# Two scatters of half rows, attention inside 64 tiles, a PSUM tile per chunk, and a residual on another engine in a two-layer float32 kernel

## The chip, the cores and the metric

The kernel runs on one core of one Trainium2 chip. The metric is the device time of one execution in microseconds (us), and of several executions the median. The engines are named as the profile names them: PE is TensorE (PEld its loading of weights), DVE is VectorE, ACT is ScalarE, POOL is GpSimd, SP is SyncE, which here issues most of the transfers. A Q behind a name (SPq, POOLq) is the engine's queue of instructions.

## What is computed

Two layers over 2048 tokens of 512 channels, all in float32. Each layer normalises x, computes a branch s and a branch g from it, and adds s * silu(g). In layer 0, s is a gated recurrence over the tokens and g an expert layer in which every token takes one of two experts. In layer 1, s is an attention whose keys are pooled over blocks of 64 tokens except for the last 256, and g is an expert layer with two shared experts and four of sixteen routed ones for each token. Cut to what matters here:

```python
x = L0_attn_x                                  # (1, 2048, 512)
xn = _layernorm(x)
s = _L0_attn_ref(xn, ...)                      # recurrence, projections Wk, Wv, Wr, then Wo
g = _silu(_L0_ffn_ref(xn, ...))                # the better of E = 2 experts, FF = 2048
x = x + s * g
xn = _layernorm(x)
s = _L1_attn_ref(xn, ...)                      # 16 heads, 28 pooled keys + the last 256
g = _silu(_L1_ffn_ref(xn, ...))                # below
x = x + s * g

def _moe_forward(u, shared_w1, ..., centroids, bias):
    flat = u.reshape(-1, d)
    h = relu(einsum('td,ndf->ntf', flat, shared_w1) + shared_b1[:, None, :])
    out = flat + einsum('ntf,nfd->td', h, shared_w2) + shared_b2.sum(0)
    scores = sigmoid(flat @ centroids.T) + bias
    vals, idx = top_k(scores, 4)               # 4 of 16 experts
    gating = vals at idx, divided by their sum
    for each expert: rout += (relu(flat @ w1 + b1) @ w2 + b2) * gating   # D_FF = 352
    return out + rout
```

## The kernel before the change

Tokens stand in 16 tiles of 128 (P = 128, NT = 16, D = 512, NC = 4 chunks of channels). A scheduler in the build orders the instructions of each engine by what depends on what and by the order in which the program emits them, so the order of emission is a wish, except where `tc.keep_in_program_order` fixes an instruction. Each engine then works through its own list in order: an instruction that waits holds up all behind it on that engine. A named tile in a pool has `bufs` buffers; a writer of a buffer waits for the readers of what stood in it. Transfers from SP go out in SP's order. The stages, in order of time:

**Start (0 to about 73 us).** The 16 tiles of x are loaded, and `norm_stats` (L121) gives mean and 1/deviation of each on VectorE with a square root on ScalarE. The loop at L222 copies both into `facts` (L229, L230), normalises in place, transposes and stores the rows. From them follow the tables that say which token goes to which of layer 0's experts; `tok` and `row_mr` (L357, L358) come last.

**Layer 0 (to about 943 us).** Two pieces of work are interleaved by hand. `pieces0` (L583) runs the expert layer on gathered rows: `rows0` (L538) gathers by an indirect transfer from GpSimd, normalises on VectorE, transposes on TensorE (L558); `up0` (L562) makes the up-projection (L567) and its activation, `down0` the down-projection (L589). `recurrence(b)` (L384) is a generator over eight blocks of 256 tokens in 22 pieces each: differences and mixes, the projections of `wk`, `wv`, `wr` (L414), scans, the normalisation. The loop at L688 takes a piece of the recurrence whenever its share of the work lags behind `pieces0`.

**Between the layers (to about 1062 us).** `carried` (L698) multiplies by Wo (L705). VectorE multiplies by the gate (L832, L838), which ScalarE makes from rows `yg` that GpSimd gathers (L825). Then, for each pair of tiles, GpSimd adds x (L847), the sum is stored to `xr1`, and VectorE normalises it (L126, L854). TensorE transposes it into `xT` (L137) and multiplies by the centroids (L863).

**Routing, shared experts, keys (to about 1350 us).** Tables place each of the 8192 answers (2048 tokens x 4) in tiles of 128 rows, each tile of one expert: 64 full ones and up to 16 more, NRT = 80; how many there are is known only while the kernel runs (`tiles_n`, 73 in this input). 64 scatters from GpSimd (L1036), two streams of them under way at a time, put the rows into `xs` in DRAM. `down_shared` (L1092) stores the shared experts' sums, with the normalised x added, into `comb` in DRAM (L1105).

**Routed tiles (1350 to about 1908 us).** The loop at L1722 runs j from 0 to 80. `hidden_rows(j)` (L1648) loads the tile's rows x and its expert's weights (704 + 512 + 192 + 2 KB), transposes (L1669), copies (L1671) and multiplies in three chunks of 128, 128 and 96 hidden channels into one PSUM tile `ph` (L1672, L1676), each followed by a ReLU on ScalarE (L935, through `relu`); VectorE makes the weight of each row and the row `to` to which its answer goes (L1694; six buffers). `down_rows` (L1697) of the tile before multiplies down into `py` (L1700); VectorE scales it into `y` (L1705; four buffers), and GpSimd scatters it with addition into `comb` (L1706). All those scatters write one tensor, so each waits until the one before has landed. From j = 65 on a step runs only if the tile exists (L1726).

**Attention** over the first 14 tiles of tokens is a generator of 42 pieces (L1589): queries (L1342), scores (L1550, L1556) with a softmax on VectorE and ScalarE (L1312), and values (L1575, L1583) that overwrite `xT`. 34 pieces are spread over the first 72 steps; the rest run behind the loop, where `close(i)` closes a tile of tokens between them: silu of its sum on ScalarE (L1757), times `xT` and plus `xo` on VectorE (L1759, L1762), store (L1763). The loads of the sums from `comb` (L1752) wait for every scatter.

The lines that the scatter rests on:

```python
        nc.vector.tensor_scalar(out=y, in0=py, scalar1=g, scalar2=None, op0=ALU.mult)      # L1705
        nc.gpsimd.indirect_dma_start(                                                     # L1706
            out=comb, out_offset=bass.IndirectOffsetOnAxis(ap=to, axis=0),
            in_=y, in_offset=None, compute_op=ALU.add,
        )
...
            if j <= FULL_TILES and min(j + 1, SPREAD) * AHEAD // SPREAD > taken:          # L1728
                next(att)
                taken += 1
```

## Time and profile before

| what | us |
|---|---|
| median of 3 runs | 1981.36 (1971.8 to 1984.02) |
| the profiled execution | 1987.46 |
| its span in the profile | 1985.8 |
| TensorE busy in the span | 1869.7 (94%) |
| VectorE, ScalarE, GpSimd busy | 779.6, 531.4, 371.4 |

The page gives, for each engine, busy time and a strip of 40 slices of 49.6 us each, a digit being the busy share in tenths; a strip of the clock granted to TensorE and one of the DMA engines' mean busy share stand beside them:

```profile
PE   5899999999999999999889999999999999999857
...
POOL 1211121120302120200621560001111121221120
PEclk9799999999999999999899999999999999999989
DMA  7647786536562535346532551028999999998944
```

Lines of instruction groups name the line, the engine, the operation, what it writes and reads, and the count; behind the bar stand the busy time in us, the mean of one in ns, and the idle time of the engine just before them with what ended it. Lines of waits name who waited for whom, the sum in us, the times and the longest. Timeline lines give the start, the duration, engine and line, and in brackets the idle time before with its releaser. A matmul in float32 appears as two records; the ends of matmuls are modelled.

### The profile page before, as it was taken

What the parts mean: (1) busy time and instruction counts of PE and PEld (TensorE: products, weight loads), DVE (VectorE), ACT (ScalarE), POOL (GpSimd) and SP (SyncE); (2) the same over time, 40 slices, a digit from 0 to 9 for tenths busy, and PEclk for the clock granted to TensorE, in tenths of its full rate; (3) what the DMA queues carried; (4) which work ended last, traced back from release to release, by engine and by line L of the source; (5) the groups of instructions that cost most, each with busy time, mean ns of one, the idle gap of its engine ahead of it and who ended that gap; (6) DMA issues with size and microseconds to landing.
All of it is one profiled execution on the core that took longest, in us unless ns stands there. A gap on an engine that the chain in (4) does not pass through costs nothing.

```text
span 1985.8 us, 23193 instructions
## 1 busy us (share of the span) xinstructions
PE 1869.7 (94%) x8107; PEld 1294.9 (65%) x8107; DVE 779.6 (39%) x1580; ACT 531.4 (27%) x1001; POOL 371.4 (19%) x293
## 2 busy tenths in 40 slices
PE   5899999999999999999889999999999999999857
PEld 4677777777877787777334644446776666676634
DVE  8444545362627263440256444502322222222117
ACT  5113132322324232321423122221222222222214
POOL 1211121120302120200621560001111121221120
PEclk9799999999999999999899999999999999999989
DMA  7647786536562535346532551028999999998944
GB/s 249 230 148 243 240 268 219 190 106 191 168 214 89 167 95 163 113 138 228 191 111 89 213 187 58 32 75 269 278 306 273 292 286 264 259 276 234 278 90 160
DMA packets 199488, 381.35 MB, mean 192 GB/s; under 512 B 15804, under 2 KB 106428, under 8 KB 198472
## 3 DMA queue, kind: packets, MB, share of 16 engines
q1 hardware_dynamic: 179800, 332.78, 50.8%
q0 software_dynamic: 18272, 45.62, 9.9%
q10 hardware_dynamic: 1296, 1.41, 0.2%
q8 instruction: 67, 1.10, 0.2%
q14 instruction: 53, 0.43, 0.1%
HBM read 294.04 MB, written 85.72 MB: 191 GB/s over the span
## 4 chain that ended last, share of the span: by engine, by line
PE 66%; DMA 21%; DVE 5%; issue 4%; POOL 2%; ACT 2%; SPq 0%; POOLq 0%; DVEq 0%; ACTq 0%
PE pg L567 23%; DMA comb<-y,to 17%; PE py L589 11%; PE proj L414 7%; PE py L1098 4%; PE ph L1676 4%; PE ph L949 3%; PE py L1700 3%; PE pw L1583 1%; PE pl L863 1%; PE pq L1342 1%; PE pw L1467 1%; PE pq L1398 1%; POOL xr L847 1%; PE po L1458 1%
## 5 line engine op out<-in xcount | busy, mean ns | idle before, releaser
L567 PE MATMUL pg<-xg,w 128*128 128x256 f32 (+1 forms) x2304 | 494.9, 367 | 0.0
L567 PEld LDWEIGHTS pg<-xg,w 128*128 128x128 f32 x2304 | 419.0, 190 | 90.1 <-issue 41.6
L1676 PEld LDWEIGHTS ph<-xg,w 128*128 128x128 f32 (+1 forms) x1776 | 224.3, 185 | 128.6 <-ACT ht L935 64.2
L1676 PE MATMUL ph<-xg,w 128*128 128x128 f32 (+1 forms) x1776 | 245.5, 282 | 29.3 <-ACT xg L1671 14.4
L589 PE MATMUL py<-wd,hT 128*128 128x512 f32 x544 | 256.9, 593 | 3.0 <-DVE hT L574 3.0
L1700 PE MATMUL py<-w,ht 128*128 128x512 f32 (+1 forms) x438 | 219.7, 602 | 0.0
L1706 POOL DMA_INDIRECT comb<-y,to x73 | 113.8, 1559 | 459.9 <-DVE to L1694 279.9
L574 DVE TENSOR_TENSOR hT<-sg,pg 128x256 f32<-128x256 f32 (+1 forms) x144 | 57.0, 401 | 329.9 <-ACT sg L572 329.8
L572 ACT ACTIVATE sg<-pg 128x256 f32<-128x256 f32 (+1 forms) x144 | 53.4, 371 | 412.2 <-PE pg L567 411.9
L935 ACT ACTIVATE ht<-ph,b1t 128x128 f32<-128x128 f32 (+1 forms) x222 | 81.1, 365 | 296.0 <-PE ph L1676 286.7
L589 PEld LDWEIGHTS py<-wd,hT 128*128 128x128 f32 x544 | 102.1, 190 | 72.2 <-issue 61.9
L1705 DVE TENSOR_SCALAR y<-py,g 128x512 f32<-128x512 f32 x73 | 54.5, 747 | 157.2 <-PE py L1700 104.6
L1694 DVE TENSOR_TENSOR to<-junk,away 128x1 int32<-128x1 f32 x74 | 11.8, 159 | 221.7 <-DMA comb<-y,to 220.9
L1098 PE MATMUL py<-w,hT 128*128 128x512 f32 (+1 forms) x192 | 89.3, 596 | 0.0
L1700 PEld LDWEIGHTS py<-w,ht 128*128 128x128 f32 (+1 forms) x438 | 72.2, 194 | 25.8 <-issue 24.4
L949 PE MATMUL ph<-xT,w 128*128 128x512 f32 (+1 forms) x192 | 88.0, 597 | 0.1
L1036 POOL DMA_INDIRECT xs<-acc,slot x64 | 63.4, 991 | 69.2 <-DMA xs<-acc,slot 45.5
L1671 ACT COPY xg<-tp 128x512 f32<-128x512 f32 x74 | 43.2, 584 | 101.6 <-PE tp L1669 99.2
L705 PE MATMUL po<-wo,yb 128*128 128x512 f32 x128 | 61.6, 637 | 8.4 <-DVE acc L838 4.4
L414 PE MATMUL proj<-xm,wk 128*128 128x256 f32 x256 | 59.4, 386 | 3.6 <-DVE xm L404 3.6
L1342 PE MATMUL pq<-xT,wqg 128*128 128x256 f32 x224 | 56.9, 390 | 5.5 <-PEq L1724 5.5
L414 PE MATMUL proj<-xm,wv 128*128 128x256 f32 x256 | 61.5, 394 | 0.0
(416 smaller groups left out, 2180.7 us busy)
## 6 DMA issues: line engine op xcount, KB each, us to landing
w<-in_w_dram SPq DMA_DIRECT2D x76, 704.0 KB
w<-in_w_dram SPq DMA_DIRECT2D x76, 512.0 KB
w<-in_w_gate_dram SPq DMA_DIRECT2D x72, 512.0 KB
w<-in_w_up_dram SPq DMA_DIRECT2D x72, 512.0 KB
wd<-in_w_down_dram SPq DMA_DIRECT2D x72, 512.0 KB
xs<-zero SPq DMA_DIRECT2D x16, 1360.0 KB
x<-xs SPq DMA_DIRECT2D x74, 272.0 KB
w<-in_w_dram SPq DMA_DIRECT2D x76, 192.0 KB
```

The lines of the kernel that those rows point to most:

```text
L414: nc.tensor.matmul(out=ps[:, j, :], lhsT=w_[:, c, (o0 + j) * P : (o0 + j + 1) * P], rhs=xm[:, c, :], start=(c == 0), stop=(c == NC - 1),)
L567: nc.tensor.matmul(out=pg[:, i, 0:n], lhsT=w[:, c, i * FH + f * P : i * FH + (f + 1) * P], rhs=xg[:, c, 0:n], start=(c == 0), stop=(c == N ...
L589: nc.tensor.matmul(out=p, lhsT=hT[:, u * P : (u + 1) * P], rhs=wd[:, f, :], start=first_, stop=last_,)
L705: nc.tensor.matmul(out=po, lhsT=yb[:, c, s * P : (s + 1) * P], rhs=wo[:, c, :], start=(c == 0), stop=(c == NC - 1),)
L935: nc.scalar.activation(dst, src, AF.Relu, bias=b)
L949: nc.tensor.matmul(out=ph[0:n, :], lhsT=up(w, f, n, c), rhs=xT[:, c, cols], start=(c == 0), stop=(c == NC - 1),)
L1036: ins = nc.gpsimd.indirect_dma_start(out=xs, out_offset=bass.IndirectOffsetOnAxis(ap=slot[:, i, k : k + 1], axis=0), in_=acc[:, i, :], in_ ...
L1098: nc.tensor.matmul(out=py, lhsT=hT[0:n, e, f, s * P : (s + 1) * P], rhs=down(w, f, n), start=(e == 0 and f == 0), stop=(e == NS - 1 and f ...
L1342: nc.tensor.matmul(out=pq[:, j, :], lhsT=w[:, c, w0 : w0 + P], rhs=xT[:, c, tc0], start=(c == 0), stop=(c == NC - 1),)
L1676: nc.tensor.matmul(out=ph[0:n, f, :], lhsT=up(w, f, n, c), rhs=xg[:, c, :], start=(c == 0), stop=(c == NC - 1),)
L1700: nc.tensor.matmul(out=py, lhsT=hT[0:n, f, :], rhs=down(w, f, n), start=(f == 0), stop=(f == NF1 - 1),)
L1706: nc.gpsimd.indirect_dma_start(out=comb, out_offset=bass.IndirectOffsetOnAxis(ap=to, axis=0), in_=y, in_offset=None, compute_op=ALU.add,)
```

## The change

The parts of it:

- `comb` becomes two tensors of 256 channels each. `down_shared` stores each tile in two transfers, `down_rows` scatters each answer by two indirect transfers from GpSimd, one into each, and the closing loads each tile in two.
- All 42 pieces of attention run in the first 64 steps, spread evenly. The loads of `xo` move to steps 48 to 63. The closing of the 16 tiles stands in one loop behind all tiles, in the order of the tokens.
- `ph` is a PSUM tile of its own for each of the three chunks, from the same pool of two buffers.
- The residual add between the layers (L847) goes from GpSimd to VectorE.
- At the start, 1/deviation is written into `facts` at once and the means are copied once for all tiles (15 small copies fewer). Seven pieces of the recurrence are emitted ahead of `pieces0`, and the first transpose of gathered rows (L558) is kept in program order.

```diff
@@ -107,7 +107,8 @@
     dram = ctx.enter_context(tc.tile_pool(name="rows", bufs=1, space=bass.MemoryType.DRAM))
     xs = dram.tile([NRT * P, DX], F32, name="xs")
 
-    comb = dram.tile([T + P, D], F32, name="comb")
+
+    comb = [dram.tile([T + P, D // 2], F32, name=f"comb{h}") for h in range(2)]
     xnt0 = dram.tile([P, NC, T], F32, name="xnt0")
     ys0 = dram.tile([NST * P, D], F32, name="ys0")
     yr0 = dram.tile([NRB, P, NC * RB], F32, name="yr0")
@@ -118,14 +119,15 @@
         i = VEC.index(name)
         return vecs[:, i, c : c + 1]
 
-    def norm_stats(src, n):
-
-        mv = small.tile([P, n, 2], F32, tag=f"mv{n}", name="mv")
+    def norm_stats(src, n, mv=None, rstd=None):
+
+        if mv is None:
+            mv = small.tile([P, n, 2], F32, tag=f"mv{n}", name="mv")
+            rstd = small.tile([P, n], F32, tag=f"rstd{n}", name="rstd")
         for i in range(n):
             st = small.tile([P, 6], F32, tag="bnst", name="st")
             nc.vector.bn_stats(out=st, in_=src[:, i, :])
             nc.vector.bn_aggr(out=mv[:, i, :], in_=st)
-        rstd = small.tile([P, n], F32, tag=f"rstd{n}", name="rstd")
         nc.scalar.activation(rstd, mv[:, :, 1], AF.Sqrt, bias=eps)
         nc.vector.reciprocal(out=rstd, in_=rstd)
         return mv, rstd
@@ -218,16 +220,15 @@
         out=eno, in0=col[:, 0:NST], scalar1=float(P), scalar2=None, op0=ALU.mult
     )
 
+    all_mv = n0.tile([P, NT, 2], F32, bufs=1, name="all_mv")
     dl = n0.tile([P, NT], F32, bufs=1, name="dl")
     for i in range(0, NT, 2):
         xin = xins[i // 2]
-        mv, rstd = norm_stats(xin, 2)
+        mv, rstd = norm_stats(xin, 2, all_mv[:, i : i + 2, :], facts[:, 2, i : i + 2])
         shift = small.tile([P, 2], F32, tag="shift", name="shift")
         nc.vector.scalar_tensor_tensor(
             out=shift, in0=mv[:, :, 0], scalar=-1.0, in1=rstd, op0=ALU.mult, op1=ALU.mult
         )
-        nc.vector.tensor_copy(facts[:, 1, i : i + 2], mv[:, :, 0])
-        nc.vector.tensor_copy(facts[:, 2, i : i + 2], rstd)
         for j in range(2):
             xn = xin[:, j, :]
             nc.scalar.activation(
@@ -246,6 +247,7 @@
     wr = rc.tile([P, NC, D], F32, name="wr")
     tc.keep_in_program_order(nc.sync.dma_start(out=wv, in_=a["Wv"]))
     tc.keep_in_program_order(nc.sync.dma_start(out=wr, in_=a["Wr"]))
+    nc.vector.tensor_copy(facts[:, 1, :], all_mv[:, :, 0])
 
     sel = n0.tile([P, NT, E0], F32, bufs=1, name="sel")
     nc.vector.tensor_scalar(
@@ -555,7 +557,9 @@
         for u, xr in enumerate(xrs):
             tp = f0t.tile([P, NC, P], F32, tag="tp", name="tp")
             for c in range(NC):
-                nc.tensor.transpose(tp[:, c, :], xr[:, c * P : (c + 1) * P], ident)
+                ins = nc.tensor.transpose(tp[:, c, :], xr[:, c * P : (c + 1) * P], ident)
+                if u == c == 0 and js[0] == 0:
+                    tc.keep_in_program_order(ins)
             nc.scalar.copy(xg[:, :, u * P : (u + 1) * P], tp)
             yield
 
@@ -685,6 +689,9 @@
     WORK = NST * NPART * NFH - SLACK
     sh = ExitStack()
     after, spent = None, 0
+    for _ in range(7):
+        next(blocks)
+        done += 1
     for amount in pieces0():
         spent += amount
         while after is None and done * WORK < spent * PIECES * NRB:
@@ -844,7 +851,7 @@
         nc.sync.dma_start(out=xr, in_=a["x"][rows2, :].rearrange("(n p) d -> p n d", p=P))
         i0 = b * n
         for s in range(n):
-            nc.gpsimd.tensor_tensor(
+            nc.vector.tensor_tensor(
                 out=xr[:, s, :], in0=xr[:, s, :], in1=acc[:, i0 + s, 0:D], op=ALU.add
             )
         nc.sync.dma_start(out=xr1[rows2, :].rearrange("(n p) d -> p n d", p=P), in_=xr)
@@ -1102,7 +1109,10 @@
                     )
             y = m1s.tile([P, D], F32, tag="y", bufs=3, name="y")
             nc.vector.tensor_tensor(out=y, in0=py, in1=acc[:, t, 0:D], op=ALU.add)
-            nc.sync.dma_start(out=comb[t * P : (t + 1) * P, :], in_=y)
+            for h, c_ in enumerate(comb):
+                nc.sync.dma_start(
+                    out=c_[t * P : (t + 1) * P, :], in_=y[:, h * D // 2 : (h + 1) * D // 2]
+                )
 
     next(block)
 
@@ -1603,7 +1613,6 @@
 
         def value(i):
             values(i, got.pop(i))
-            finished.append(i)
 
         for b in range(nb - 1):
             q = start(b)
@@ -1669,15 +1678,15 @@
             nc.tensor.transpose(tp[:, c, :], x[:, c * P : (c + 1) * P], ident)
         xg = m1x.tile([P, NC, P], F32, tag="xg", name="xg")
         nc.scalar.copy(xg, tp)
-        ph = m1ps.tile([P, NF1, P], F32, tag="ph", name="ph")
         hT = hts[j % len(hts)]
         for f, n in enumerate(FCH):
+            ph = m1ps.tile([P, P], F32, tag="ph", name="ph")
             for c in range(NC):
                 nc.tensor.matmul(
-                    out=ph[0:n, f, :], lhsT=up(w, f, n, c), rhs=xg[:, c, :],
+                    out=ph[0:n, :], lhsT=up(w, f, n, c), rhs=xg[:, c, :],
                     start=(c == 0), stop=(c == NC - 1),
                 )
-            relu(hT[0:n, f, :], ph[0:n, f, :], b1t[0:n, j, f : f + 1])
+            relu(hT[0:n, f, :], ph[0:n, :], b1t[0:n, j, f : f + 1])
 
         junk = m1x.tile([P, NR], F32, tag="junk", name="junk")
         g = m1x.tile([P, 1], F32, tag="g", name="g")
@@ -1703,16 +1712,16 @@
             )
         y = m1x.tile([P, D], F32, tag="y", bufs=4, name="y")
         nc.vector.tensor_scalar(out=y, in0=py, scalar1=g, scalar2=None, op0=ALU.mult)
-        nc.gpsimd.indirect_dma_start(
-            out=comb, out_offset=bass.IndirectOffsetOnAxis(ap=to, axis=0),
-            in_=y, in_offset=None, compute_op=ALU.add,
-        )
+
+        for h, c_ in enumerate(comb):
+            nc.gpsimd.indirect_dma_start(
+                out=c_, out_offset=bass.IndirectOffsetOnAxis(ap=to, axis=0),
+                in_=y[:, h * D // 2 : (h + 1) * D // 2], in_offset=None, compute_op=ALU.add,
+            )
 
     FULL_TILES = T * KR // P
-    AHEAD = 34
-    SPREAD = FULL_TILES + NR // 2
-    finished = []
-    att = attention()
+    att = list(range(6 * (FULL[0] * P // QB)))
+    attend = attention()
     rest_of = {}
     held = nc.values_load(
         tiles_n[0:1, 0:1], min_val=FULL_TILES, max_val=NRT,
@@ -1721,39 +1730,36 @@
     pending, taken = None, 0
     for j in range(NRT + 1):
 
-        with contextlib.ExitStack() as step:
+        with contextlib.ExitStack() as more:
             if j > FULL_TILES:
-                step.enter_context(tc.If(held > j - 1))
+                more.enter_context(tc.If(held > j - 1))
             made = hidden_rows(j) if j < NRT else None
-            if j <= FULL_TILES and min(j + 1, SPREAD) * AHEAD // SPREAD > taken:
-                next(att)
+            if taken < len(att) and (j + 1) * len(att) // FULL_TILES > taken:
+                next(attend)
                 taken += 1
             if pending is not None:
                 down_rows(*pending)
             pending = (j, *made) if made is not None else None
-        if j > FULL_TILES and min(j + 1, SPREAD) * AHEAD // SPREAD > taken:
-            next(att)
-            taken += 1
-        i = j - (NRT - NT)
-        if 0 <= i < NT:
-            xo = fin.tile([P, D], F32, tag="xo", name="xo")
-            nc.sync.dma_start(out=xo, in_=xr1[i * P : (i + 1) * P, :])
-            rest_of[i] = xo
+            i = j - (FULL_TILES - NT)
+            if 0 <= i < NT:
+                xo = fin.tile([P, D], F32, tag="xo", name="xo")
+                nc.sync.dma_start(out=xo, in_=xr1[i * P : (i + 1) * P, :])
+                rest_of[i] = xo
+    assert next(attend, None) is None
 
     tiles.close()
     fin2 = ctx.enter_context(tc.tile_pool(name="fin2", bufs=NT))
 
 
     sums_of = {}
-    early = list(FULL) + list(finished)
-    todo = early + [i for i in range(NT) if i not in early]
-    for i in todo:
+    for i in range(NT):
         y = fin2.tile([P, D], F32, tag="y", name="y")
-        nc.sync.dma_start(out=y, in_=comb[i * P : (i + 1) * P, :])
+        for h, c_ in enumerate(comb):
+            nc.sync.dma_start(
+                out=y[:, h * D // 2 : (h + 1) * D // 2], in_=c_[i * P : (i + 1) * P, :]
+            )
         sums_of[i] = y
-
-    def close(i):
-        y = sums_of[i]
+    for i, y in sums_of.items():
         nc.scalar.activation(y, y, AF.Silu)
         y4 = y.rearrange("p (c t) -> p c t", t=P)
         nc.vector.tensor_tensor(
@@ -1761,15 +1767,6 @@
         )
         nc.vector.tensor_tensor(out=y, in0=y, in1=rest_of[i], op=ALU.add)
         nc.sync.dma_start(out=a["out"][i * P : (i + 1) * P, :], in_=y)
-
-    closed = 0
-    for u, _ in enumerate(att):
-        if u >= 2:
-            for i in early[closed : closed + 2]:
-                close(i)
-                closed += 1
-    for i in todo[closed:]:
-        close(i)
 
 
 # ---- launch: one core; the host lays the inputs out, and adds what the shapes alone decide ----
```

## The prediction

> **What bounds the kernel now.** I read the page's slices first, then the waits of the stretch in which the routed tiles run, then stretches, then the timeline where a stall stood out. TensorE is busy 94% of the span, so a change counts only where it takes work or a stall off TensorE, or shortens the end, where TensorE waits. The routed tiles run from 1350 to 1908 us, the end from there to 1985.8. In the slices the DMA is nearly full there too, but two other lines tell more:
>
> ```profile
> L1706 POOL DMA_INDIRECT comb<-y,to x73 | 113.8, 1559 | 459.9 <-DVE to L1694 279.9 <-DMA comb<-y,to 95.9 <-DMA w<-in_w_dram 15.6
> ...
> L1036 POOL DMA_INDIRECT xs<-acc,slot x64 | 63.4, 991 | 69.2 <-DMA xs<-acc,slot 45.5 <-DVE acc L1027 19.6 <-issue 4.1
> ```
>
> The 73 scatters of answers (L1706) occupy GpSimd for 114 us and idle it for 460: each waits until the one before has landed, since all add into one tensor. Issues run from 1368.1 to 1924.6, 7.7 us apart on the mean. Who waits behind it, between 1355 and 1846:
>
> ```profile
> POOL comb L1706 <- DVE to L1694: 265.7, 43, 8.0
> ...
> DVE to L1694 <- DMA comb<-y,to: 212.8, 45, 8.3
> ...
> PE ph L1676 <- ACT xg L1671: 14.4, 4, 6.4
> ```
>
> `to` has six buffers; when the scatters fall behind, VectorE stands at L1694 until an old one lands. How that reaches TensorE, once per softmax that is caught behind it:
>
> ```profile
> 1493.73 0.16 DVE L1694 TENSOR_TENSOR to<-junk,away 128x1 int32<-128x1 f32 x1 [7.35 <-DMA comb<-y,to]
> ...
> 1495.02 0.28 ACT L1319 ACTIVATE near<-near 128x96 f32<-128x96 f32 x1 [7.01 <-DVE near L1318]
> 1495.21 0.35 ACT L935 ACTIVATE ht<-ph,b1t 128x128 f32<-128x128 f32 x1
> ...
> 1495.61 2.02 PE L1676 MATMUL ph<-xg,w 128*96 128x128 f32 x8 [4.56 <-ACT ht L935]
> ```
>
> VectorE waits for the scatter, ScalarE for VectorE's softmax, the ReLU stands behind it on ScalarE, and TensorE idles 4.56 us; its next eight matmuls take 2.02 us where 1.05 is usual. Stretches (columns: length, PE, PEld, DVE, ACT, POOL busy, clock, DMA share, GB/s):
>
> ```profile
> 1355.00:1460.00 105.00, 104.20 (x588) 74.51 (x588) 29.80 (x106) 28.52 (x67) 17.26 (x12) 1.00 0.99 306
> 1460.00:1680.00 220.00, 209.05 (x1175) 152.88 (x1174) 54.13 (x189) 53.24 (x129) 43.55 (x29) 0.97 0.94 279
> 1680.00:1846.00 166.00, 157.80 (x849) 110.92 (x848) 40.81 (x141) 40.21 (x95) 34.37 (x22) 0.98 0.90 263
> ```
>
> So the 65 unconditional steps (to 1846) are TensorE's, less 0.8 + 11.0 + 8.2 = 20 us idle and 0.03 x 220 + 0.02 x 166 = 10 us of clock: 30 us. The conditional tiles after 1846:
>
> ```profile
> 1862.04 0.97 PEld L1676 LDWEIGHTS ph<-xg,w 128*128 128x128 f32 x8 [0.71 <-ACT ht L935]
> ...
> 1863.72 0.90 PEld L1676 LDWEIGHTS ph<-xg,w 128*96 128x96 f32 x8 [0.71 <-ACT ht L935]
> ...
> 1864.67 1.88 PE L1700 MATMUL py<-w,ht 128*128 128x512 f32 x4
> ...
> 1872.02 1.88 PE L1700 MATMUL py<-w,ht 128*128 128x512 f32 x4
> ```
>
> One step is 7.35 us, and in it TensorE waits 0.71 us twice for a ReLU to free the PSUM tile that all three chunks share. The end:
>
> ```profile
> 1924.62 1.55 POOL L1706 DMA_INDIRECT comb<-y,to  x1 [4.05 <-DMA comb<-y,to]
> 1932.77 8.54 SPq L1752 DMA_DIRECT2D y<-comb  x16
> ...
> 1938.05 0.69 DVE L1759 TENSOR_TENSOR y<-xT,y 128x512 f32<-128x512 f32 x1 [16.25 <-ACT y L1757]
> ...
> 1939.13 1.08 PEld L1556 LDWEIGHTS ps<-kd_geo,qg 128*128 128x128 f32 x4 [15.96 <-DVE qg L1355]
> ...
> 1981.79 0.69 DVE L1762 TENSOR_TENSOR y<-y,xo 128x512 f32<-128x512 f32 x1
> ```
>
> The last answer product ends near 1904.6, but the last scatter is issued 20 us later, the sums are loaded at 1932.8, and the attention left over waits behind the closing rows and runs to 1980.
>
> **The change, part by part** (against the profiled span, 1985.8; that execution took 1987.46, 6.1 above the median 1981.36).
>
> *Scatter in halves.* In the built order each half waits only for the same half of the tile before, so two are under way. GpSimd issues 2 x 1.56 = 3.1 us a tile, beside other work (it does nothing else there); `y` and `to` are freed when both land. The packet records give a 2 KB scatter packet 178 ns at the median, plain loads of 2 KB 84 and of 1 KB 46; so a 1 KB scatter packet should take about 2 x 46 + 8 = 100, and 16 instead of 8 per DMA engine add 16 x 0.100 - 8 x 0.178 = 0.2 us a tile (bounds 0 and, if nothing is saved by size, 8 x 0.178 = 1.4). How long a pair takes is not in the trace. From below: L1036, two streams without addition, 113 us for 64, so 3.5 us a pair. From above: two whole scatters one behind the other, 2 x 7.7 = 15.4. Nearest is the whole scatter, 7.7 under load and 5.6 at the end with the weights gone: half the packets take some 0.7 us off, so about 7.1 a pair, the second overlapping. A tile of TensorE's work will be 7.9 us (below), so the chain falls off the path; of the 30 us I keep 5 for waits on x and weights: -25.
> The Trainium skill, "DMA: Bandwidth & Descriptors", Anatomy of one DMA — SWDGE (gpsimd) path, speaks against halves: 2.0 us fixed plus bytes / 436e3. By it a half would take 2.3 us and a whole 2.6, so a pair in series would cost 1.77 wholes, here 13.6 us a tile, and the end (by the formula of the third rival below) some 385 us later; what speaks against it is that the waits let the halves overlap. The whole scatter's 5.6 us without other traffic is well over the page's 2.6.
>
> *Attention inside the 64 tiles.* Stretches taken line by line give TensorE's attention work after 1908 as 13.1 (L1342) + 12.3 (L1550) + 7.0 (L1556) + 2.4 (L1575) + 14.8 (L1583) = 49.6 us, at clock 0.72 to 0.94; at full clock about 46. All of it enters the 64 tiles: +46 there. Its VectorE and ScalarE parts lie under TensorE (VectorE is busy a quarter of that stretch). Loads of `xo`, 16 x 256 KB, move there too: 4.2 MB at 306 GB/s = 14 us of DMA spread over 510; hidden while DMA has room (280 of 306 GB/s used now). Without room it costs 14.
>
> *Up-projection in own tiles.* The third chunk waits for the first ReLU, 1.67 us after the chunk's start; two chunks take 1.72. So the two waits of 0.71 go: 7.35 to 5.95. But a step loads 1.41 + 0.28 MB and scatters 0.26, and 1.95 MB at 306 GB/s is 6.4 us; three tiles are loaded ahead. I take 6.2: 8 x 1.15 = -9. In the first 64 most of these waits are covered by products of the tile before: -3.
>
> *The end.* Main stage: 1846 + 46 - 25 - 3 = 1864. Eight conditional steps: 1904.6 - 1846 - 9 = 49.6, so the last product at 1913.6. Answer 0.75 and a handover 0.4, then two issues (1.6): 1916.4; then 8.15 from last issue to the loads (1924.62 to 1932.77), and 1.5 for what has queued: loads at 1926. To the first VectorE row 5.3 (1932.77 to 1938.05). 16 tiles x two operations of 0.68, pitched 1.21 a tile in the trace where four stand together: the last starts 18.7 later. From there 4.0 to the span's end (1981.79 to 1985.8). Sum 1954. SP issues 32 loads and 16 stores at 0.53 each, 25.4 from 1926, and some 3 to land: 1954.8, no lower. So 1955. Nothing covers this end any more: 30 us in which TensorE stands.
>
> *Residual on VectorE.* GpSimd's 16 adds take 1.27 us each, VectorE's same shape 0.66 (L838); VectorE waits 21.9 us for them (L126), TensorE idles 8.8 + 6.6 us from 943 to 1062. VectorE is busy 31.6 of 77 us there, so 16 x 0.66 = 10.6 fits. GpSimd's gathers of `yg` no longer stand between adds. Bounds: -15, all that TensorE idles there; +10.6, if those 16 operations lay bare. In the steady part a pair of tiles takes TensorE 7.37 us for 7.13 of work, so there is little to gain there and most at the stage's start: -6.
>
> *Recurrence first, copies.* TensorE waits 9.5 us at 66.3 for the first gathered rows. In the built order 21 projections (products of L414, 2 x 0.216 = 0.43 us) now stand ahead of the first L567 instead of behind it, in that idle time; TensorE is full from 100 to 480, so all counts: -9, 0 if the first L567 (72.9) comes as much later. I take -8. Sixteen small VectorE copies less: 16 x 0.08 = 1.3 us, inside this. The two 128 KB stores per tile instead of one are SP's, which has room.
>
> Sum: 1955 - 6 - 8 = 1941; 1941 / 1985.8 x 1981.36 = 1937, say 1938.
>
> **Rivals.**
> *The DMA engines become the bound* in the main stage. For: share 0.90 to 0.99 already. Against: 306 GB/s was reached with TensorE at 104.2 of 105. At the upper packet bound the stage needs 64 x 1.4 = 90 us of DMA more, and 14 for `xo`; free are 0.06 x 491 = 30 and the 18 by which the stage grows: +56, 1994. Halfway between the bounds: 1966, which I take.
> *The stalls stay*, through softmax on VectorE and ScalarE rather than scatters: +25, 1963. Against: each long stall has a wait for comb ahead of it.
> *The halves go one behind the other* (other side: slower). Loads then at 1368 + 72 P + 8 for a pair of P us, the end 29 later, less 14: 1985.8 is passed at P = 8.26. With P = 9.3 (7.7 plus an issue) the end is 2061. For: one queue carries both. Against: the waits are separate, and packets take only 2 to 3 us of the 7.7.
> *The halves change nothing* (P stays 7.7): the tile's 7.9 matches it, backlog grows only in the conditional steps, 8 x (7.7 - 6.2) = 12: 1950. That is no loss, and lies in the forecast's range.
>
> **How the numbers follow.** Forecast, with P up to 7.7 and TensorE setting the main stage: 0.72; its own range is 1918 (residual at -15, first part at -9, no stall kept, an end 5 shorter) to 1961 (first part and residual gain nothing, conditional steps stay at 7.35). DMA or stalls: 0.16, 1961 to 1994. Halves in series: 0.12, 1985 to 2061. The range 1914 to 1985 leaves out the last case and the extremes of the others. One per cent, about what a measurement here can tell from no change, is 19.8 us: faster is below 1961.6, slower above 2001.2. Faster: 0.72 and a little of the second case, 0.74; same: the rest of the second and the near end of the third, 0.16; slower 0.10.
>
> **What would show it.** Right: two scatter issues a tile, pairs under 7.9 us apart; no wait of VectorE at `to` for comb; clock 1.00 from 1460 on; conditional steps near 6.2; last scatter within 12 us of the last product; loads to end 29 us; first L567 near 72 with fewer L414 behind it. Wrong: pairs over 8.3 us; TensorE waiting for weights; a closing of over 40 us.

## The result, and the profile after

| | before | after |
|---|---|---|
| median of 4 runs each, side by side (us) | 1977.81 (1971.8 to 1984.02) | 1951.73 (1949.3 to 1956.27) |
| profiled execution, its span | 1987.46, 1985.8 | 1949.3, 1947.6 |

The ratio is 0.9874, 95% interval 0.9851 to 0.9898: 1.3% faster. The forecast was 1938, with 1914 to 1985 as its range, so the time lies inside it, with 26 of the 43 us that were forecast as the gain. The two profiled executions lie 38 us apart, since that of before was slower than all four of its runs and that of after the fastest of its four, so a few us between the columns below can belong to the run and not to the change. The moments that the prediction's sum passes through, in us of the span (predicted ones with -14 for the first part and the residual already in them):

| moment | before | predicted | after |
|---|---|---|---|
| first product of the routed up-projection | 1359.3 | 1345 | 1348.2 |
| 65 steps done | 1846 | 1850 | 1846.8 |
| last answer product ends | 1904.6 | 1899.6 | 1893.3 |
| last scatter issued | 1924.6 | 1902.4 | 1909.3 |
| first load of sums | 1932.8 | 1912 | 1917.6 |
| end of the span | 1985.8 | 1941 | 1947.6 |

TensorE's work was done 6 us earlier than forecast, and the scatters ended 7 us later. The strips of the page of the changed kernel, and its two groups of scatters (L1717 was L1706, L1043 was L1036):

```profile
PE   5899999999999999999989999999999999999990
...
PEclk9899999999999999999999999999999999999995
...
L1717 POOL DMA_INDIRECT comb<-y,to x146 | 227.4, 1557 | 343.0 <-DMA comb<-y,to 140.5
...
L1043 POOL DMA_INDIRECT xs<-acc,slot x64 | 63.0, 985 | 67.1 <-DMA xs<-acc,slot 42.8
```

146 issues of 1.56 us stand in the place of 73. The releaser that the group names first is now the scatter itself, where before it was VectorE's `to`. That name misled, as two lines of the kernel before show:

```profile
1516.19 0.16 DVE L1694 TENSOR_TENSOR to<-junk,away 128x1 int32<-128x1 f32 x1 [1.04 <-DMA comb<-y,to]
...
1516.83 1.55 POOL L1706 DMA_INDIRECT comb<-y,to  x1 [7.97 <-DVE to L1694]
```

VectorE woke on the landing of a scatter (at 1516.1 by the trace's landing events), and GpSimd issued the next one 0.73 us after the same landing; `to` only happened to end in between. In 68 of its 72 waits the kernel before issued a scatter 0.73 us or little more after the landing of the one before. So its chain was bound by landings from end to end, as the prediction took it to be. In the waits of the changed kernel between 1355 and 1846, these lines name `comb` or `to` (now L1703); no line has VectorE waiting for a scatter, where before it stood 212.8 us:

```profile
POOL comb L1717 <- DMA comb<-y,to: 114.8, 32, 6.5
...
POOL comb L1717 <- DVE to L1703: 37.6, 10, 4.9
```

The stretches of the changed kernel (columns as before: length, PE, PEld, DVE, ACT, POOL busy, clock, DMA share, GB/s):

```profile
1355.00:1460.00 105.00, 105.00 (x603) 77.17 (x603) 33.23 (x111) 26.93 (x65) 42.60 (x28) 1.00 1.01 303
1460.00:1680.00 220.00, 220.00 (x1235) 160.94 (x1233) 65.67 (x215) 58.10 (x138) 91.43 (x60) 1.00 0.98 281
1680.00:1846.00 166.00, 165.97 (x869) 116.48 (x868) 46.85 (x142) 40.53 (x94) 62.02 (x40) 1.00 0.85 238
```

TensorE is busy 491 of 491 us at full clock: the 20 us of idle time and 10 us of lost clock that the prediction counted are gone. Two answer products of the changed kernel, one conditional step apart, in its timeline:

```profile
1872.69 1.88 PE L1709 MATMUL py<-w,ht 128*128 128x512 f32 x4
...
1875.74 2.92 PE L1685 MATMUL ph<-xg,w 128*128 128x128 f32 x24
...
1878.50 1.88 PE L1709 MATMUL py<-w,ht 128*128 128x512 f32 x4
```

A step is 5.81 us instead of 7.35, and the 24 matmuls of the three chunks now run as one block without a wait for a ReLU. The end of the changed kernel:

```profile
1854.47 1.55 POOL L1717 DMA_INDIRECT comb<-y,to  x1 [3.39 <-DVE to L1703]
...
1893.22 1.55 POOL L1717 DMA_INDIRECT comb<-y,to  x1 [4.91 <-DMA comb<-y,to]
1893.34 0.75 DVE L1714 TENSOR_SCALAR y<-py,g 128x512 f32<-128x512 f32 x1 [4.53 <-PE py L1709]
...
1907.23 1.55 POOL L1717 DMA_INDIRECT comb<-y,to  x1 [0.30 <-issue]
1909.28 1.55 POOL L1717 DMA_INDIRECT comb<-y,to  x1 [0.49 <-DMA comb<-y,to]
1917.61 15.09 SPq L1758 DMA_DIRECT2D y<-comb  x32
...
1922.76 1.29 DVE L1765 TENSOR_TENSOR y<-xT,y 128x512 f32<-128x512 f32 x2 [28.67 <-DMA y<-comb]
...
1940.83 1.28 DVE L1768 TENSOR_TENSOR y<-y,xo 128x512 f32<-128x512 f32 x2
```

The last answer is ready at 1894.1 (1893.34 + 0.75), but eight halves go out from 1893.2 on, the last at 1909.3. From the first load to the end are 30.0 us (29 forecast), 19.3 of them VectorE's rows from 1922.8 to 1942.1.

### The profile page after: what moved, and what is told of

Same layout as the page of the kernel before. It is cut to its first block, busy times and chain, and to the rows that moved or that the text cites. A ratio compares the mean times of both kernels' runs of the same rounds, so it can differ in the third digit from the quotient of the medians.

```text
span 1947.6 us, 23278 instructions
## 1 busy us (share of the span) xinstructions
PE 1846.0 (95%) x8107; PEld 1287.3 (66%) x8107; DVE 784.7 (40%) x1581; ACT 527.8 (27%) x997; POOL 466.1 (24%) x350
## 4 chain that ended last, share of the span: by engine, by line
PE 84%; DMA 6%; DVE 3%; issue 2%; POOL 2%; ACT 2%; SPq 1%; DVEq 0%; POOLq 0%; ACTq 0%
PE pg L571 23%; PE py L593 12%; PE ph L1685 9%; PE py L1709 9%; PE proj L416 7%; PE py L1105 4%; PE ph L956 3%; DMA comb<-y,to 3%; PE pq L1352 2%; PE pw L1593 2%; PE tp L1678 1%; PE ps L1560 1%; PE po L712 1%; PE ps L1566 1%; PE pl L870 1%
## 5 line engine op out<-in xcount | busy, mean ns | idle before, releaser
L1717 POOL DMA_INDIRECT comb<-y,to x146 | 227.4, 1557 | 343.0 <-DMA comb<-y,to 140.5
L1685 PEld LDWEIGHTS ph<-xg,w 128*128 128x128 f32 (+1 forms) x1776 | 202.3, 182 | 37.6 <-ACT xg L1680 31.4
L1685 PE MATMUL ph<-xg,w 128*128 128x128 f32 (+1 forms) x1776 | 213.9, 277 | 1.6 <-DMA w<-in_w_dram 1.6
L1709 PE MATMUL py<-w,ht 128*128 128x512 f32 (+1 forms) x438 | 207.6, 593 | 0.0
L1709 PEld LDWEIGHTS py<-w,ht 128*128 128x128 f32 (+1 forms) x438 | 76.7, 191 | 56.2 <-issue 54.0
L1043 POOL DMA_INDIRECT xs<-acc,slot x64 | 63.0, 985 | 67.1 <-DMA xs<-acc,slot 42.8
L416 PE MATMUL proj<-xm,wr 128*128 128x256 f32 x256 | 60.5, 391 | 4.3 <-ACT v L452 4.3
L464 POOL TENSOR_TENSOR ex<-st_p,qt 128x1024 f32<-128x1024 f32 x8 | 18.3, 2288 | 193.0 <-DVE qt L463 193.0
L1678 PEld LDWEIGHTS tp<-ident,x 128*128 128x128 f32 x296 | 36.7, 140 | 38.8 <-issue 20.8
L545 POOL DMA_INDIRECT xr<-in_x_dram,tok x17 | 23.2, 1367 | 160.3 <-PE tp L560 133.2
```

Source lines behind the costliest of these rows:

```text
L416: nc.tensor.matmul(out=ps[:, j, :], lhsT=w_[:, c, (o0 + j) * P : (o0 + j + 1) * P], rhs=xm[:, c, :], start=(c == 0), stop=(c == NC - 1),)
L1043: ins = nc.gpsimd.indirect_dma_start(out=xs, out_offset=bass.IndirectOffsetOnAxis(ap=slot[:, i, k : k + 1], axis=0), in_=acc[:, i, :], in_ ...
L1685: nc.tensor.matmul(out=ph[0:n, :], lhsT=up(w, f, n, c), rhs=xg[:, c, :], start=(c == 0), stop=(c == NC - 1),)
L1709: nc.tensor.matmul(out=py, lhsT=hT[0:n, f, :], rhs=down(w, f, n), start=(f == 0), stop=(f == NF1 - 1),)
L1717: nc.gpsimd.indirect_dma_start(out=c_, out_offset=bass.IndirectOffsetOnAxis(ap=to, axis=0), in_=y[:, h * D // 2 : (h + 1) * D // 2], in_of ...
```

## The experiments

The theory after the result was still the forecast's: halves take the scatter chain off TensorE's path. Its rival: the halves change nothing, and it is the attention that gives the chain its time. Each kernel ran beside runs of the kernel before, to which its ratio is taken; the medians of those runs lie between 1977.8 and 1980.6, so a difference of a few us between two rows of the table has to be seen in the ratios or the profiles too. A number that all share tells how fast a chain went: the time from the first to the last scatter issue, over 72 tiles. It is put beside each time here.

| kernel | us, median (range) | ratio to before (95%) | first to last issue, per tile |
|---|---|---|---|
| before | 1977.81 | | 556.6, 7.73 |
| after | 1951.73 | 0.9874 (0.9851 to 0.9898) | 554.6, 7.70 |
| after, one scatter | 1951.21 (1946.72 to 1953.65) | 0.9868 (0.9851 to 0.9885) | 556.3, 7.73 |
| after, one PSUM tile | 1954.94 (1951.34 to 1960.66) | 0.9882 (0.9861 to 0.9903) | 556.1, 7.72 |
| before, halves alone | 1957.82 (1954.99 to 1959.73) | 0.9900 (0.9883 to 0.9918) | 526.6, 7.31 |
| before, attention alone | 1959.47 (1953.31 to 1964.3) | 0.9895 (0.9869 to 0.9922) | 561.4, 7.80 |
| after, residual on GpSimd | 1960.31 (1959.68 to 1962.14) | 0.9898 (0.9875 to 0.9921) | 555.9, 7.72 |
| after, no pieces ahead | 1950.49 (1948.27 to 1953.93) | 0.9854 (0.9828 to 0.9881) | 553.0, 7.68 |
| attention over 72 steps | 1937.62 (1935.61 to 1941.25) | 0.9787 (0.9760 to 0.9814) | 534.7, 7.43 |
| the same, one scatter | 1964.66 (1955.14 to 1973.69) | 0.9916 (0.9884 to 0.9949) | 566.7, 7.87 |
| over 72, attention kept ahead of the closing | 1934.03 (1933.18 to 1937.15) | 0.9778 (0.9742 to 0.9815) | 534.5, 7.42 |
| the same, 5 adds on GpSimd | 1940.70 (1938.44 to 1942.31) | 0.9803 (0.9766 to 0.9839) | 532.7, 7.40 |

**The changed kernel with whole scatters.**

```diff
-    comb = [dram.tile([T + P, D // 2], F32, name=f"comb{h}") for h in range(2)]
+    comb = dram.tile([T + P, D], F32, name="comb")
...
-        for h, c_ in enumerate(comb):
-            nc.gpsimd.indirect_dma_start(
-                out=c_, out_offset=..., in_=y[:, h * D // 2 : (h + 1) * D // 2], ...
-            )
+        nc.gpsimd.indirect_dma_start(out=comb, out_offset=..., in_=y, ...)
```

> The changed kernel with one sum tensor, one scatter of 512 channels for each answer and one load for each tile of sums; all else as changed. Theory 'halves' (the pair keeps up where the whole scatter does not): a tile of TensorE's work is now 7.67 us, a whole scatter 7.7 us under load, so the chain is level with TensorE at best; the waits of VectorE at `to` and stalls of TensorE come back, some 15 to 25 us in the main stage, and the time is 1965 to 1977. Rival 'attention' (42 pieces among 64 tiles alone gave the chain its time, the pair is no faster than the whole): main stage within 4 us of the changed kernel's, the time 1948 to 1956.

Measured 1951.21: no difference from the changed kernel's 1951.73. Its waits and stretches over the same time:

```profile
POOL comb L1712 <- DMA comb<-y,to: 227.4, 38, 8.7
...
POOL comb L1712 <- DVE to L1700: 37.9, 6, 8.4
```

```profile
1355.00:1460.00 105.00, 105.00 (x602) 77.21 (x601) 34.28 (x115) 27.01 (x65) 20.42 (x13) 1.00 1.00 306
1460.00:1680.00 220.00, 220.00 (x1236) 161.15 (x1236) 64.72 (x211) 57.91 (x137) 44.95 (x29) 1.00 0.94 279
1680.00:1846.00 166.00, 165.97 (x866) 116.09 (x866) 47.53 (x143) 40.33 (x93) 31.00 (x20) 1.00 0.82 240
```

GpSimd waits longer for each scatter, but VectorE has no wait for one, and TensorE stands nowhere: 65 steps of 7.67 us (1348.2 to 1846.8 after) are nearly as long as a whole scatter takes, 7.73, and the buffers take up the rest. In the order of the changed kernel the halves are worth nothing. The forecast's theory falls.

**Each of the two alone, in the kernel before.** The halves as in the diff of the change:

> The kernel before with two sum tensors and scatters of 256 channels alone. Theory 'halves': stalls in the main stage go, the conditional stage starts 15 to 25 us earlier (1825 against 1846) and loads of the sums follow by as much; the attention left over covers the lag: 1953 to 1965. Rival 'attention': the pair takes what the whole took, no change within 5 us of before: 1973 to 1983. Other side (two DMAs cost more than one): 1990 or more.

And the attention with the closing as in the change, all else as before:

> The kernel before with all 42 pieces of attention in the 64 full tiles, the loads of the old x there, and the closing in one loop; whole scatters, one PSUM tile, GpSimd's residual. Theory 'halves': stalls stay, since they come from the scatter and not from the tile's length: main stage end 1846 + 46 = 1892, last product 1951, sums loaded some 20 later, closing 30: 1985 to 2000. Rival 'attention': tiles of 7.6 to 7.9 us let a scatter of 7.7 keep up, so the stalls of 30 us go: main stage end 1862 to 1866, last product 1921 to 1925, loads 12 to 20 later, closing 30: 1965 to 1975.

Measured 1957.82 and 1959.47: either one alone gains about 20 us. A wait and a stretch of the halves alone:

```profile
DVE to L1697 <- DMA comb<-y,to: 180.6, 45, 7.5
```

```profile
1460.00:1680.00 220.00, 214.04 (x1217) 156.72 (x1217) 59.51 (x209) 55.14 (x134) 91.75 (x59) 0.98 0.99 298
1680.00:1846.00 166.00, 162.84 (x888) 114.07 (x887) 39.79 (x137) 43.08 (x101) 71.93 (x47) 1.00 0.97 272
```

and the same of the attention alone:

```profile
DVE to L1693 <- DMA comb<-y,to: 31.0, 11, 5.4
```

```profile
1460.00:1680.00 220.00, 219.80 (x1240) 160.67 (x1240) 67.66 (x219) 56.60 (x135) 43.41 (x28) 1.00 0.94 279
1680.00:1846.00 166.00, 165.83 (x872) 115.50 (x870) 46.44 (x144) 41.55 (x95) 34.10 (x22) 1.00 0.84 241
```

With halves in the old order the chain is still the bound: VectorE still waits 180.6 us at `to`. But a pair takes 7.31 us against 7.73 for a whole, so the chain is 30 us shorter. With the attention inside the 64 tiles TensorE stands 0.4 us in these two stretches: a longer tile hides a scatter of the old speed. The attention alone removes all 30 us of stalls, and its time is 6 us below even the band of the rival; the halves alone remove about two thirds (the 65 steps take 467.7 us instead of 486.5; 6 us of idle time and 4 of clock are left in them, and the other 3 us of idle time in the two stretches stand behind 1824, in conditional steps), and the attention that is left over covers their lag at the end.

**One PSUM tile for the three chunks.**

```diff
+        ph = m1ps.tile([P, NF1, P], F32, tag="ph", name="ph")
         for f, n in enumerate(FCH):
-            ph = m1ps.tile([P, P], F32, tag="ph", name="ph")
...
-                    out=ph[0:n, :], ...
+                    out=ph[0:n, f, :], ...
```

> The changed kernel with one PSUM tile for the three chunks of the up-projection, as before. Theory 'TensorE sets the end': the conditional step goes back from 5.8 to 7.35 us, 8 x 1.5 = 12 us, and the main stage loses 3: 1967. Rival 'the scatter chain sets the end' (the last scatter was issued 16 us after the last product, so TensorE has slack there): conditional steps 7.35 us but the last scatter at most 3 to 5 us later, the lag behind the last product about 5 us: 1954 to 1958.

Measured 1954.94, 3.2 more, which is within the spread of the runs. A step and the last scatter of this kernel:

```profile
1863.91 1.88 PE L1709 MATMUL py<-w,ht 128*128 128x512 f32 x4
...
1871.27 1.88 PE L1709 MATMUL py<-w,ht 128*128 128x512 f32 x4
...
1915.61 1.55 POOL L1717 DMA_INDIRECT comb<-y,to  x1 [0.39 <-DMA comb<-y,to]
```

In the profile the conditional steps are 7.35 us again and the last product starts 17.9 us later (1910.6 for 1892.7), but the last scatter only 6.3 later (1915.6 for 1909.3), and the routed stage had begun 2.6 later. From the start of the last product to the last scatter it is 5.0 us instead of 16.6. At the end the chain of scatters is the bound, and most of TensorE's gain in the conditional steps disappears into its backlog.

**The residual back on GpSimd.** The one word `vector` of the diff becomes `gpsimd`.

> The changed kernel with the residual add between the layers back on GpSimd. Theory 'residual' (the step was mis-sized, it is worth the 10.7 us by which the time from the last up-projection to the last centroid product fell): the last centroid product comes 9 to 11 us later and the time is 1960 to 1963. Rival 'prediction's size': 6 us, 1957 to 1959. Rival 'clock' (the gain there comes from the clock, 0.98 for 0.93, whatever the residual does): under 3 us.

Measured 1960.31, 8.6 more by the medians. By the ratios, each taken to its own runs of the kernel before, it is 0.0024 or 4.7 us, and their intervals overlap. Two waits of this kernel between 943 and 1062, neither of which the changed kernel has:

```profile
POOL xr L854 <- DVE acc L845: 26.2, 10, 5.1
...
DVE st L129 <- POOL xr L854: 23.2, 13, 4.7
```

VectorE makes `acc`, GpSimd adds x to it, and VectorE needs the sum for its statistics: the chain crossed twice between engines for each tile. From the last up-projection of layer 0 to the last centroid product the kernel before takes 109.8 us, this one 108.0, the changed one 100.2. The other profiles bear it out: the four kernels here with the add on GpSimd take 108.0 to 110.0 us, 109.3 on the mean, the eight with it on VectorE 99.7 to 103.6, 101.9 on the mean. So the residual is worth about 7.5 us there. The rival 'clock' falls: at the same clock of 0.97 from 943 to 1062 the changed kernel with whole scatters takes 99.7 us and this one 108.0. Between 'prediction's size' (6) and 'residual' (10.7) these runs do not decide.

**Without the seven pieces ahead.**

```diff
-    for _ in range(7):
-        next(blocks)
-        done += 1
...
-                if u == c == 0 and js[0] == 0:
-                    tc.keep_in_program_order(ins)
```

> The changed kernel without the seven pieces of the recurrence ahead of the expert layer and without the transpose held in order (16 small copies less are kept). Theory 'the start gives and takes' (9.5 us of idle filled, first up-projection 7.8 us later): first up-projection near 73, last one 1 to 3 us later than with the pieces, 1952 to 1955. Rival 'prediction's size': the last up-projection 8 us later, 1959 to 1961. Rival 'the pieces cost': it is 3 us or more faster, 1945 to 1949.

Measured 1950.49, no difference from the changed kernel. What the pieces do is seen in TensorE's timeline of the changed kernel,

```profile
52.65 9.95 PE L416 MATMUL proj<-xm,wv 128*128 128x256 f32 x32
66.87 6.23 PE L416 MATMUL proj<-xm,wr 128*128 128x256 f32 x16 [4.27 <-ACT v L452]
72.94 0.60 PE L560 MATMUL tp<-ident,xr 128*128 128x128 f32 x4
...
80.75 9.55 PE L571 MATMUL pg<-xg,w 128*128 128x256 f32 x43 [3.75 <-ACT xg L563]
```

and without them:

```profile
53.15 3.63 PE L416 MATMUL proj<-xm,wv 128*128 128x256 f32 x10
65.50 1.08 PE L560 MATMUL tp<-ident,xr 128*128 128x128 f32 x4 [8.71 <-POOL ex L465]
...
70.86 10.52 PE L569 MATMUL pg<-xg,w 128*128 128x256 f32 x48
```

An idle stretch of 8.7 us is filled, and the first up-projection comes 9.9 us later, for the most part because the pieces bring waits of their own (4.27 and 3.75 us). The last up-projection stands at 942.1 with them and at 941.0 without; over all profiles here it is 942.1 to 946.2 in the eight kernels with the pieces ahead and 941.0 to 943.6 in the four without. Nothing is gained.

**Attention over 72 steps.** If the chain sets the end, and a pair is faster than a whole wherever answers come soon enough, then shorter tiles early on should make the halves pay.

```diff
+    SPREAD = FULL_TILES + NR // 2
...
-            if taken < len(att) and (j + 1) * len(att) // FULL_TILES > taken:
+            if j <= FULL_TILES and min(j + 1, SPREAD) * len(att) // SPREAD > taken:
                 next(attend)
                 taken += 1
...
+        if j > FULL_TILES and min(j + 1, SPREAD) * len(att) // SPREAD > taken:
+            next(attend)
+            taken += 1
```

> The changed kernel with the 42 pieces of attention spread over the first 72 steps, those beyond step 64 between the conditional blocks; scatters in halves. A chain of pairs that was never short of answers issued 146 scatters in 526.6 us (halves alone in the kernel before), 7.31 us a pair; a chain of whole scatters took 556.3 (one scatter in the changed kernel), 7.73. Theory 'the chain sets the end, and halves are worth 0.42 us a tile where answers come soon enough': TensorE ends where it did, near 1893, the last scatter follows it by 4 to 8 us instead of 16, and the time is 1940 to 1946. Rival 'fixed lag' (the lag is the four buffers of y emptying, whatever the order): 1950 to 1954.

> The same with one sum tensor and whole scatters. Theory 'chain': 72 x 7.73 = 556 us from the first issue at 1353, so the last scatter stays at 1909 and the time at 1949 to 1954, 8 us or so behind the halves. Rival 'order alone' (the spread helps, halves do not): within 2 us of the halves' time. Rival 'stalls': the chain again holds up VectorE at `to`, and TensorE ends 5 to 15 us later: 1955 to 1965.

Measured 1937.62 with halves and 1964.66 with whole scatters: 27 us between two kernels whose counterparts in the order of the change did not differ. The first lies 2 us below the band of 'chain', the second at the end of that of 'stalls'. A wait and two stretches of the one with whole scatters:

```profile
DVE to L1700 <- DMA comb<-y,to: 143.9, 33, 8.8
```

```profile
1460.00:1680.00 220.00, 213.84 (x1203) 156.68 (x1203) 59.23 (x206) 55.77 (x134) 43.19 (x28) 0.99 0.94 281
1680.00:1846.00 166.00, 159.91 (x853) 114.95 (x852) 47.76 (x146) 38.75 (x90) 33.52 (x22) 0.98 0.84 242
```

The same two stretches with halves:

```profile
1460.00:1680.00 220.00, 220.00 (x1256) 161.69 (x1255) 64.07 (x214) 58.40 (x139) 93.65 (x61) 1.00 1.01 293
1680.00:1846.00 166.00, 166.00 (x898) 118.64 (x898) 47.55 (x150) 40.49 (x94) 67.22 (x43) 1.00 0.92 259
```

With whole scatters the stalls are back: a whole scatter does not fit the shorter tile. With halves TensorE has none, the chain is 20 us shorter than after, and the last scatter goes out at 1891.5. It was not the shorter lag that was expected (it is 13 us): the scheduler put the pieces meant for between the conditional steps behind all of them. That costs in the closing, as this kernel's timeline shows:

```profile
1902.60 1.28 ACT L1767 ACT_TABLE_LOAD   x1 [20.34 <-DMA y<-comb]
...
1906.91 6.42 PE L1593 MATMUL pw<-vo,sT 128*128 128x512 f32 x8 [14.83 <-ACT sT L1590]
```

ScalarE stood 20.3 us at the first silu's table for the sums, and a copy that TensorE's attention needed stood behind it.

**The leftover attention ahead of the closing.** Each silu and first product of the closing is kept in program order:

```diff
-        nc.scalar.activation(y, y, AF.Silu)
+        tc.keep_in_program_order(nc.scalar.activation(y, y, AF.Silu))
...
-        nc.vector.tensor_tensor(
+        tc.keep_in_program_order(nc.vector.tensor_tensor(
             out=y4, in0=xT[:, :, i * P : (i + 1) * P], in1=y4, op=ALU.mult
-        )
+        ))
```

> The kernel with attention over 72 steps (1937.6 us), in which the closing's silus and first products are kept behind the attention on ScalarE and VectorE. There the pieces left over (14.7 us of TensorE) stood interleaved with the closing: ScalarE waited 20.3 us at the first silu for the sums while copies of attention stood behind it, and VectorE did two softmaxes of some 4 us between closing rows. Theory 'order': the leftover attention runs under the lag of the scatters, from 1882 to about 1903, the closing then takes 30 us from the loads as in the changed kernel instead of 35.8: 1930 to 1935. Rival 'no gain': the attention's own chain of handovers ends later than the loads, 1905 or more, and the silus start as much later: 1936 to 1942.

Measured 1934.03, the lowest median here, 0.9778 (0.9742 to 0.9815) of before. The 3.6 us below the kernel without it (0.9787) are within the spread of the runs; what the profile shows is the closing. From the loads to the end are 33.6 us (1898.7 to 1932.3) instead of 35.8. Half of the rival holds too: the attention's handovers last until 1905.8, so the first silu's table is loaded 7.0 us after the first load of sums (3.2 after the change).

**Five of the sixteen last adds on GpSimd.**

```diff
-        nc.vector.tensor_tensor(out=y, in0=y, in1=rest_of[i], op=ALU.add)
+        add = nc.gpsimd if i % 3 == 1 else nc.vector
+        add.tensor_tensor(out=y, in0=y, in1=rest_of[i], op=ALU.add)
```

> The same with the last add of 5 of the 16 closing tiles on GpSimd, which is idle there (1.27 us each; 0.6 on VectorE). Theory 'VectorE sets the closing' (32 operations pitched 1.21 us a tile, 19.3 us): 3 us less than without, 1927 to 1932. Rival 'loads and stores set it' (SP issues 32 loads in 15 us and 16 stores in 8.5 behind them): within 1.5 us of the kernel without.

Measured 1940.70, slower, which neither side expected. A stretch of its closing:

```profile
1923.79 1.64 POOL L1773 TENSOR_TENSOR y<-y,xo 128x512 f32<-128x512 f32 x1 [2.56 <-DMA out_dram<-y]
1924.35 1.64 DVE L1773 TENSOR_TENSOR y<-y,xo 128x512 f32<-128x512 f32 x1
1925.90 0.68 DVE L1769 TENSOR_TENSOR y<-xT,y 128x512 f32<-128x512 f32 x1
```

VectorE's add takes 1.64 us instead of 0.69 when it starts inside GpSimd's (1923.79 to 1925.43). Each add that is given away saves VectorE some 0.6 us, and VectorE's next one takes 0.95 longer. From VectorE's first row of the closing to its last are 21.7 us (1913.28 to 1935.02) against 20.6 without (1907.72 to 1928.36): 1.1 us lost instead of 3 gained. The rest of the 6.7 us is not the adds': 5.4 stand in this profile ahead of the routed tiles (first product at 1354.8 for 1349.4), where the two programs have the same order and the granted clock differed (0.96 for 1.00 from 943 to 1062). Whether that holds for the timed runs too stays open.

## Why the prediction was right or wrong

**The sign and the size of the main stage: right, for the wrong reason.** The sum said 46 us of attention in, 25 us of stalls and 3 us for the PSUM tiles out. From the first routed product to step 65 it is 486.5 us before (1359.3 to 1845.8) and 498.7 after; 486.5 + 46 - 30 - 2.9 = 499.6, where 2.9 is what one PSUM tile for the three chunks adds to this stretch (501.6). All 30 us of stalls went. But the step that gave the credit to the halves failed, at "so about 7.1 a pair ... so the chain falls off the path". A pair took 7.31 us where it was the bound, and the whole scatter's 7.73 would have done: TensorE's tile grew to 7.67 us by the attention. The prediction had that number before it (a tile of 7.9 against a whole scatter of 7.7) and drew from it only a rival, "the halves change nothing", with 1950 for its time. That rival is what the chip did; whole scatters in the changed kernel give 1951.21. Halves and longer tiles are two cures for one stall, about 20 us each alone, and the second one adds nothing.

**The pair.** The mechanism was right, two under way and less than one whole; the size was not: 0.42 us off a whole, where 0.7 was taken. The landing events show the same: between 1355 and 1846 a half lands 6.69 us after its issue on the mean (halves alone in the kernel before), a whole 7.11 (the kernel before).

**The end: the step from last product to last scatter failed.** "Answer 0.75 and a handover 0.4, then two issues" gave 2.8 us; it is 16.0 (1893.3 to 1909.3). The sum took the chain to have no backlog there, although its own pair of 7.1 us is longer than its own step of 6.2. The step became even shorter, 5.8, and under the weights' loads five pairs took 38.75 us (issues at 1854.47 to 1893.22), 7.75 each. In these five steps the lag of a pair's first issue behind its answer grew from 6.9 to 16.6 us, 5 x (7.75 - 5.8); the last three pairs, with the loads gone, went out 4.7 us apart and took 3.4 of it back. So the PSUM tiles' 12 us in the conditional steps, where 9 were forecast, are worth about 3 to the end, no more than the spread of the runs.

**Residual.** 6 us forecast, about 7.5 measured in the profiles (4.7 by the ratios, 8.6 by the medians): no miss that these runs can show. The bound of 15 held; about a third of VectorE's waits for GpSimd (21.9 us before) turned into time.

**Recurrence first.** Mis-sized: 8 forecast, nothing measured. Of the two bounds named (9, and 0 if the first up-projection comes as much later) the second held.

**Closing.** 29 us from the loads to the end; 30.0 measured.

**The rivals.** DMA as the bound: its share was 0.98 to 1.01 up to 1680, and TensorE did not wait. The packets bear it out: a 1 KB scatter packet took 102 ns at the median, for 100 estimated, a 2 KB one 178. Stalls through softmax: none was left. Halves one behind the other: two were under way; 7.31 us a pair is less than one whole scatter. The rule weighed there, of the Trainium skill ("DMA: Bandwidth & Descriptors", Anatomy of one DMA — SWDGE (gpsimd) path: 2.0 us fixed plus bytes / 436e3), gives 1.77 wholes as an estimate for the two halves in series; the runs show 0.95 of a whole in the kernel before. A fixed cost that overlaps is not paid twice.

**The sum.** Against the span of the profiled execution it came out 6.6 us short, and that it is no more is luck. Missing were 13.2 at the last scatter, 6.8 in the first part and 1.0 in the closing, 21 us; too much by 6.1 in the main stage (5 of stalls kept that did not stay), 3.1 in the conditional steps, 3.6 in the residual (in this profile) and some 1.6 in smaller steps, 14 us. Against the medians, 1951.73 for 1938, it is 14 us short.

**What stays open.** Under load nearly all of a pair's 7.3 to 7.75 us is the landing, 6 to 7 us from the issue, and 0.73 us to the next issue. Its packets need 16 x 0.102 = 1.6 us of each DMA engine. What the rest of the landing is made of was not taken apart.

## What to carry to other kernels

When one change carries two cures for the same wait, work out the time with each alone: if one alone makes the waiting stage longer than the resource it waits for, the other is worth nothing there, and may be worth 27 us in another order. Compare the pace of a chain with the pace of its producer stage by stage; where the producer is faster (here 5.8 against 7.75 us), the backlog is the term that sets the end, and speeding up the producer there gains little. Filling an idle stretch is a gain only if what stood behind it does not come later by as much.

## What the runs showed of the hardware

VectorE and GpSimd held each other up: an add of two operands in SBUF took VectorE 1.64 us while GpSimd did one, 0.69 otherwise, and GpSimd's took 1.64 where the same shape took 1.27 between the layers. This agrees with the Trainium skill ("SBUF — State Buffer", Who interferes with whom), by which a VectorE instruction with two inputs in SBUF contends with a GpSimd one that reads SBUF.

Without the weights' loads, at the end, halves went out 2.3 us apart on the mean (eight from 1893.22 to 1909.28), so 4.6 a pair; whole scatters there went out 5.7 apart (1903.39, 1909.21, 1914.99, 1920.61 in the kernel with whole scatters over 72 steps). A whole scatter landed there 4.7 to 5.0 us after its issue (kernel before), against 7.11 on the mean under load. With two halves under way a good part of the landing is hidden.
